# Values of two key blocks together, another order of inversions and masks, and a rearranged end in a two-layer graph network

## The chip, the cores and the metric

One core of a Trainium2 chip runs the whole program. The metric is device time of one execution in microseconds (us), the median of several. Engines are called as the profile calls them: PE is TensorE's matmul, PEld its weight load, DVE VectorE, ACT ScalarE, POOL GpSimd.

## The reference, cut to what matters

```python
# x: (32, 512, 512) float32, adj: (512, 512) of 0 and 1; 8 heads of 64
x = layernorm(x + deg * (x @ Wi.T + b) + adj @ (x @ Wj.T))     # layer 0
q, k, v = (x @ W.T + b for W, b in ...)                        # layer 1, per head
scores = q @ k.T / 8, with -inf where adj == 0
x = layernorm(x + softmax(scores) @ v @ Wo.T + bo)
```

The attention runs over 512 keys, taken as four blocks of 128.

## The kernel before

Everything is float32. The kernel is a hand-made pipeline: while the attention of one batch runs, TensorE also works on the layers of its neighbours. A **period** is one batch's attention, in eight **steps**: two groups of four heads (g = 0, 1), four key blocks each (kc). Each step has scores, values of the step before, and then **pieces**: the projections of other batches, in 8 or 16 matmul passes each, with seven products where eight would be usual.

```python
psum: mm_tile("a"), mm_tile("b")      # one bank each, for pieces
      ov_tile()  bufs=2               # one bank each, values of one head group
      sc_tile()  bufs=2               # two banks each: scores, row sums, last accumulators

def scores(b, hp, kc):                # two heads
    ps = sc_tile()
    for s in range(2):
        matmul(ps[:, s, :], KT[...64 rows...], QT[...])
    e = E[hp % 2, kc] = work([P, 2, N], "e", 4)
    nc.scalar.activation(ps, ps, AF.Exp, scale=QSCALE)       # in place, ACT
    nc.vector.tensor_tensor(e, ps, edge[...], op=OP.mult)    # the mask, DVE

def values(b, g, kc):                 # 32-column matmuls into the two ov tiles
def sums(g, ...):                     # row sums: 32-column matmuls with ones, into an sc tile
def drain(b, g):                      # ACT: sums from PSUM to SBUF
def rest(b, g):                       # DVE: four reciprocals, two scalings, one reduction
    return [(invert, g, c) for c in range(4)] + [(scale, b, g, 0), (scale, b, g, 1), (tell, b, g)]

for step in range(8):
    g, kc = divmod(step, 4)
    scores(b, 2 * g, kc); scores(b, 2 * g + 1, kc)           # with exponentials and masks
    values(pb, pg, pk)                                       # of the step before
    if pk == 3:
        sums(pg); drain(pb, pg); extra = rest(pb, pg)
    for f in PERIODS[n][step]:                               # the pieces and their helpers
        run(f)
        # after a piece: all of extra in step 0, one of it in step 4
    # ... (cuts throughout)
```

A piece ends with its **eviction**: DVE (or ACT) reads its bank (in this text the kernel's word for one 128x512 float32 tile of `psum`) and adds it into the result. The next piece but one uses that bank again.

## Time and profile before

| | before |
|---|---|
| median of the first 3 runs, us | 3696.0 (3695.5 to 3696.7) |
| PE busy | 99% |
| DVE / POOL / ACT busy | 65% / 53% / 28% |
| a period of eight steps (mean of periods 2 to 30), us | 113.46 |

The period is taken from the trace: from the first scores matmul of its first step to that of the next period. "Busy" is the union of an engine's instructions over the span. A busy share of 99% on one engine and no waits in the steady part mean that whatever costs this engine time costs the program time. The lines that carry this are in the prediction.

### The profile page before, as it was taken

What the parts mean: (1) busy time and instruction counts of PE and PEld (TensorE: products, weight loads), DVE (VectorE), ACT (ScalarE), POOL (GpSimd) and SP (SyncE); (2) the same over time, 40 slices, a digit from 0 to 9 for tenths busy, and PEclk for the clock granted to TensorE, in tenths of its full rate; (3) what the DMA queues carried; (4) which work ended last, traced back from release to release, by engine and by line L of the source; (5) the groups of instructions that cost most, each with busy time, mean ns of one, the idle gap of its engine ahead of it and who ended that gap; (6) DMA issues with size and microseconds to landing.
All of it is one profiled execution on the core that took longest, in us unless ns stands there. A gap on an engine that the chain in (4) does not pass through costs nothing.

```text
span 3693.0 us, 49640 instructions
## 1 busy us (share of the span) xinstructions
PE 3662.9 (99%) x18470; PEld 2510.3 (68%) x18470; DVE 2393.1 (65%) x3134; ACT 1028.6 (28%) x1483; POOL 1940.0 (53%) x1985
## 2 busy tenths in 40 slices
PE   9999999999999999999999999999999999999998
PEld 6766667676767676767676767676767666666663
DVE  4666666666666666666666666666666666666665
ACT  2232232222222223222223222223232322222322
POOL 3555545556445555455554555644555545555443
PEclk9999999999999999999999999999999999999999
DMA  8445556444555445564555544455545555445541
GB/s 258 141 120 140 138 154 160 139 131 135 151 157 151 129 135 146 152 165 125 135 140 151 162 144 128 136 150 155 158 123 138 142 158 159 134 133 139 148 138 44
DMA packets 797173, 530.02 MB, mean 144 GB/s; under 512 B 530432, under 2 KB 611840, under 8 KB 796928
## 3 DMA queue, kind: packets, MB, share of 16 engines
q1 hardware_dynamic: 780384, 494.78, 49.7%
q10 hardware_dynamic: 16320, 31.46, 2.3%
q8 instruction: 151, 2.47, 0.3%
q14 instruction: 94, 0.77, 0.1%
q0 software_dynamic: 224, 0.53, 0.0%
HBM read 453.25 MB, written 73.40 MB: 143 GB/s over the span
## 4 chain that ended last, share of the span: by engine, by line
PE 97%; DVE 1%; POOL 0%; DMA 0%; ACT 0%; SPq 0%; issue 0%; DVEq 0%; ACTq 0%; POOLq 0%
PE mma L436 31%; PE mmb L436 31%; PE sc L490 13%; PE ov L512 12%; PE mmb L334 4%; PE mma L334 3%; PE sc L522 2%; PE mmb L611 0%; PE mma L611 0%; DVE e L495 0%; DVE rl L531 0%; DMA xa<-hd 0%; SPq L376 0%; PE sc L736 0%; DVE st L298 0%
## 5 line engine op out<-in xcount | busy, mean ns | idle before, releaser
L494 ACT ACTIVATE sc<-sc 128x1024 f32<-128x1024 f32 x512 | 493.0, 1007 | 1554.8 <-PE sc L490 1548.8
L495 DVE TENSOR_TENSOR e<-sc,edge 128x1024 f32<-128x1024 f32 x512 | 602.6, 1218 | 205.8 <-ACT sc L494 173.3
L436 PE MATMUL mmb<-ring,big 128*128 128x256 f32 x3144 | 731.7, 381 | 0.0
L436 PE MATMUL mma<-ring,big 128*128 128x256 f32 x3112 | 724.4, 381 | 1.5 <-DVE xh L454 0.8
L436 PEld LDWEIGHTS mmb<-ring,big 128*128 128x128 f32 x3144 | 591.9, 190 | 131.6 <-issue 27.7
L436 PEld LDWEIGHTS mma<-ring,big 128*128 128x128 f32 x3112 | 585.8, 190 | 132.3 <-issue 26.5
L405 POOL TENSOR_TENSOR big<-big 128x512 f32<-128x512 f32 x376 | 492.4, 1339 | 34.5 <-DVE big L382 14.3
L490 PE MATMUL sc<-q,k 64*128 64x512 f32 x2048 | 509.4, 615 | 0.0
L512 PE MATMUL ov<-e,v 128*32 128x512 f32 x4096 | 492.4, 598 | 4.6 <-DVE oT L547 4.6
L501 POOL TENSOR_TENSOR es<-e 128x1024 f32<-128x1024 f32 x128 | 300.8, 2361 | 350.2 <-DVE e L495 350.2
L436 PE MATMUL mma<-big,ring 128*128 128x256 f32 x1808 | 430.3, 381 | 0.0
L436 PE MATMUL mmb<-big,ring 128*128 128x256 f32 x1776 | 422.8, 381 | 1.0 <-DVE v L465 1.0
L300 POOL TENSOR_SCALAR mv<-mv 128x1 f32<-128x1 f32 x256 | 49.8, 194 | 674.2 <-DVE mv L299 661.9
L436 PEld LDWEIGHTS mma<-big,ring 128*128 128x128 f32 x1808 | 340.5, 190 | 73.0 <-issue 26.0
L436 PEld LDWEIGHTS mmb<-big,ring 128*128 128x128 f32 x1776 | 334.3, 190 | 73.4 <-issue 26.0
L512 PEld LDWEIGHTS ov<-e,v 128*32 128x32 f32 x4096 | 106.9, 109 | 351.9 <-issue 320.8
L204 POOL TENSOR_TENSOR xlo<-xh,xhi 128x512 fp32r<-128x512 f32 x128 | 162.7, 1283 | 338.1 <-ACT xhi L203 338.1
L490 PEld LDWEIGHTS sc<-q,k 64*128 64x128 f32 x2048 | 176.3, 186 | 208.2 <-issue 207.0
L349 POOL TENSOR_TENSOR big<-big,deg_r 128x512 f32<-128x512 f32 x124 | 173.5, 1400 | 263.5 <-DVE big L348 263.5
L503 DVE TENSOR_TENSOR es<-es,e 128x1024 f32<-128x1024 f32 x250 | 304.8, 1220 | 0.0
L454 DVE TENSOR_TENSOR xh<-xh,mma 128x512 f32<-128x512 f32 x186 | 126.7, 681 | 263.9 <-PE mma L436 263.9
L454 DVE TENSOR_TENSOR xh<-xh,mmb 128x512 f32<-128x512 f32 x186 | 126.7, 681 | 259.2 <-PE mmb L436 259.2
(161 smaller groups left out, 3663.6 us busy)
## 6 DMA issues: line engine op xcount, KB each, us to landing
ring<-wo SPq DMA_DIRECT2D x217, 256.0 KB, 2.8
ring<-wq SPq DMA_DIRECT2D x160, 256.0 KB, 3.9
ring<-wv SPq DMA_DIRECT2D x160, 256.0 KB, 3.4
ring<-wk SPq DMA_DIRECT2D x160, 256.0 KB, 3.3
ring<-wi SPq DMA_DIRECT2D x155, 256.0 KB, 2.7
ring<-wj SPq DMA_DIRECT2D x155, 256.0 KB, 2.6
xh<-in_x_dram SPq DMA_DIRECT2D x32, 1024.0 KB, 5.4
xa<-in_x_dram SPq DMA_DIRECT2D x124, 256.0 KB, 4.0
```

Of the source, the lines that this page charges most:

```text
L204: nc.gpsimd.tensor_sub(lo, xs, hi.bitcast(FT))
L334: nc.tensor.matmul(pm, parts[w][:, jc, :], adjR[:, jc, :], start=(w == 0 and jc == 0), stop=(w == 1 and jc == NC - 1))
L349: nc.gpsimd.tensor_tensor(XD[b][:, dc, :], XD[b][:, dc, :], deg_r, op=OP.mult)
L405: nc.gpsimd.tensor_tensor(dst, p, q, op=OP.subtract)
L436: nc.tensor.matmul(pm[:, c * Q:(c + 1) * Q], lhs, rhs, start=first, stop=(kc == 1 and n == len(terms) - 1), skip_group_check=True)
L454: nc.vector.tensor_tensor(d, d, pm, op=OP.add)
L490: nc.tensor.matmul(ps[:, s, :], KT[b, hp // 2][r, hp % 2, kc * P:(kc + 1) * P], QT[b, hp // 2][r, hp % 2, :], start=True, stop=True)
L494: nc.scalar.activation(ps, ps, AF.Exp, scale=QSCALE)
L495: nc.vector.tensor_tensor(e, ps, edge[:, kc:kc + 1, :].to_broadcast([P, 2, N]), op=OP.mult)
L501: nc.gpsimd.tensor_add(ES[i], E[i, 0], E[i, 1])
L503: nc.vector.tensor_add(ES[i], ES[i], E[i, kc])
L512: nc.tensor.matmul(PV[g][r][32 * h:32 * h + 32, :], V[b][:, kc, c0:c0 + 32], E[h // 2, kc][:, h % 2, :], start=(kc == 0), stop=(kc == NC - 1))
```

## The change

The intent is to spare TensorE changes of kind. Values are made for two key blocks together, ahead of the scores of every second step. As sums and inversions then come ahead of the scores in the first step of a group, DVE's work there is put in a new order: inversions first, then the pieces' evictions, then the masks. In step 0 the masks come behind all pieces: the loop runs what stands in `late` only `if some`, and there `some = len(extra)`, which is 0 once the inversions have run. In step 4 one mask follows each of the first two pieces. The end of the program is rearranged too. The core of the diff:

```diff
     def scores(b, hp, kc):
         ...
+        nc.scalar.activation(ps, ps, AF.Exp, scale=QSCALE)
+        SC[hp] = ps
+    def mask(hp, kc):
+        ps = SC.pop(hp)
         e = E[hp % 2, kc] = work([P, 2, N], "e", 4)
-        nc.scalar.activation(ps, ps, AF.Exp, scale=QSCALE)
         nc.vector.tensor_tensor(e, ps, edge[...], op=OP.mult)
@@ the loop
-            scores(b, 2 * g, kc)
-            scores(b, 2 * g + 1, kc)
-            ... values(pb, pg, pk), sums, drain
+            alone = b == B - 1 and step > 0
+            if alone: ... scores and masks first, as before
+            if alone or kc % 2 == 0:
+                for pb, pg, pk in due:
+                    values(pb, pg, pk)
+                    if pk == NC - 1: ... sums, drain, extra = rest(pb, pg)
+                due = []
+            due.append((b, g, kc))
+            if not alone:
+                for i in range(2):
+                    scores(b, 2 * g + i, kc)
+                if kc == 0:
+                    for f in extra:            # inversions ahead of the pieces
+                        f[0](*f[1:])
+                    extra = []
+                    late = [(mask, 2 * g + i, kc) for i in range(2)]   # masks behind
+                else:
+                    for i in range(2):
+                        mask(2 * g + i, kc)
@@ phase_b: apply and store of the first half one piece earlier
@@ last batch: two key pieces moved into it, its last two pieces into step 4,
@@ the last accumulators in score tiles of their own, sums drained before the inversions
```

More of the change, by code (lines that the diff above doesn't have):

```diff
@@ L481, in piece @@
                     nc.vector.scalar_tensor_tensor(d[:, c], pm[:, c, :], bc, p1[:, c, :], op0=OP.add, op1=OP.add)
-    E, ES, PV, RL = {}, {}, {}, {}
+    SC, E, ES, PV, RL = {}, {}, {}, {}, {}
     def scores(b, hp, kc):
@@ L527, in drain, with invert @@
         nc.scalar.activation(RL[g][1], RL[g][0], AF.Identity, accum_out=told[:, j:j + 1])
-    def invert(g, part, src=1):
+    def invert(g, part):
         c = slice(part * P, (part + 1) * P)
-        nc.vector.reciprocal(RL[g][1][:, c], RL[g][src][:, c])
+        nc.vector.reciprocal(RL[g][1][:, c], RL[g][1][:, c])
     def tell(b, g):
@@ L535, in tell @@
         nc.vector.reduce_sum(told[:, j:j + 1], RL.pop(g)[1], axis=AX.X)
-    def tell_all(b, g):
-        pl, rl = RL.pop(g)
-        j = 2 * (b * 2 + g)
-        nc.gpsimd.memset(told[:, j + 1:j + 2], 0.0)
-        nc.vector.tensor_tensor_reduce(pl, pl, rl, 1.0, 0.0, OP.add, OP.add, told[:, j:j + 1])
     def scale(b, g, r, c=slice(0, N)):
@@ L568, in gnn_attention_kernel @@
     LATE = (5, 3, 6, 7, 4)
-    ALONE = ((1, "a"), (6, "b"), (2, "a"), (7, "b"), (5, "a"), (4, "b"), (3, "a"))
     def banks(n):
@@ L578, in phase_a @@
         if n == B:
-            return [pc("k", n - 1, i, bank) for i, bank in ((6, K), (5, A), (7, K), (3, A), (4, K))]
+            return [pc("k", n - 1, i, bank) for i, bank in ((5, A), (6, K), (3, A))]
         xq, aq = lambda j, m: quarter(XD[n], j, m), lambda j, m: quarter(AX_T[n], j, m)
@@ L647, in phase_b @@
         return [l0[2], *project(m, 1), l0[6], *project(m, 2), l0[7], z(add_bo, n - 1, 0), *project(m, 6), l0[4], z(stats, n, 0),
-                *project(m, 7), z(apply, n, 0), z(h_store, n, 0), l0[5], z(h_load, n, 0), z(add_bo, n - 1, 1), *project(m, 4),
+                z(apply, n, 0), z(h_store, n, 0), *project(m, 7), l0[5], z(h_load, n, 0), z(add_bo, n - 1, 1), *project(m, 4),
                 l0[3], z(stats, n, 1), z(h_turn, n, 0), *project(m, 5)]
@@ L708, in last_steps @@
         m = B - 2
-        p = {i: pc("pj", m, i, bank) for i, bank in ALONE}
+        A, K = banks(B)
+        p = {i: pc("pj", m, i, K if i in (6, 7, 4) else A) for i in ORDER}
         c = [z(combos, TO, m, ot_quarter(m), (1, 2)), z(combos, TO, m, ot_quarter(m), (3, 4))]
         own = [(4 * GA, last_part, c, 0) for c in range(2)]
-        return [[z(last_load), FLUSH, c[0], p[1], c[1]], [p[2], p[6]], [p[5], p[7], z(add_bo, B - 1, 0), z(add_bo, B - 1, 1)],
-                [p[3], p[4], z(stats, m, 0), z(stats, m, 1)], [z(apply, m, 0), z(apply, m, 1), z(store, m)], [own[0]], [own[1]], []]
+        k = [pc("k", B - 1, i, K) for i in (7, 4)]
+        return [[z(last_load), k[0], FLUSH, c[0], p[1], c[1], k[1]], [p[2], p[6]], [p[5], p[7], z(add_bo, B - 1, 0), z(add_bo, B - 1, 1)],
+                [], [p[3], p[4]], [own[0], z(stats, m, 0), z(stats, m, 1)], [own[1], z(apply, m, 0), z(apply, m, 1), z(store, m)], []]
     def run(f):
@@ L729, in last_part @@
             else:
-                t = sc_tile()
-                ACC[2], ACC[3] = t[:, 0, :], t[:, 1, :]
+                ACC[ic] = sc_tile()[:, 0, :]
         for ic in (range(2 * half, 2 * half + 2) if ic is None else (ic,)):
@@ L778, in gnn_attention_kernel @@
             g, kc = divmod(step, NC)
-            scores(b, 2 * g, kc)
-            scores(b, 2 * g + 1, kc)
-            pb, pg, pk = (b, *divmod(step - 1, NC)) if step > 0 else (b - 1, 1, NC - 1)
-            if pb >= 0:
-                values(pb, pg, pk)
-                if pk == NC - 1:
-                    sums(pg, *(((1, 3), 3) if pb == B - 1 else ()))
-                    drain(pb, pg)
-                    extra = rest(pb, pg)
-            late = [(presum, i, kc) for i in range(2) if kc > 0]
+            alone = b == B - 1 and step > 0
+            if alone:
+                for i in range(2):
[4 more added lines that the diff above has]
+                    values(pb, pg, pk)
+                    if pk == NC - 1:
+                        sums(pg, *(((1, 3), 3) if pb == B - 1 else ()))
+                        drain(pb, pg)
+                        extra = rest(pb, pg)
+                due = []
+            due.append((b, g, kc))
+            late = [(presum, i, kc) for i in range(2) if kc > 0]
+            if not alone:
+                for i in range(2):
+                    scores(b, 2 * g + i, kc)
+                if kc == 0:
[4 more added lines that the diff above has]
+                else:
+                    for i in range(2):
+                        mask(2 * g + i, kc)
             if b == B - 1 and kc > 2 - g:
@@ L808, in gnn_attention_kernel @@
     sums(1, (3,), 3)
-    for c in range(2):
-        last_part(c, 1)
+    drain(B - 1, 1)
     for ic in range(NC):
         c = slice(ic * P, (ic + 1) * P)
-        invert(1, ic, 0)
+        invert(1, ic)
         scale(B - 1, 1, 0, c)
         scale(B - 1, 1, 1, c)
+        if ic < 2:
+            last_part(0, 1, ic + 2)
+            last_part(1, 1, ic + 2)
         last_part(2, ic=ic)
@@ L819, in gnn_attention_kernel @@
             last_rows(ic - 1)
-    tell_all(B - 1, 1)
+    tell(B - 1, 1)
     last_rows(NC - 1)
```

## The prediction

Marked cuts take out what no trace or run of this case shows: rules on the engines and their memory, and with them the amount that rival (c) put on a wait and its total. The forecast's own sum: 3696 - 16 + 68 + 31 + 6 - 5 = 3780, put at 3778.

> **What bounds the kernel now.** I read the page first: busy time and the chain that ended last. One engine fills the span.
>
> ```profile
> PE 3662.9 (99%) x18470; PEld 2510.3 (68%) x18470; DVE 2393.1 (65%) x3134; ACT 1028.6 (28%) x1483; POOL 1940.0 (53%) x1985
> ...
> PE 97%; DVE 1%; POOL 0%; DMA 0%; ACT 0%; SPq 0%; issue 0%; DVEq 0%; ACTq 0%; POOLq 0%
> ```
>
> TensorE (PE) is busy 3662.9 of 3693.0 us and is 97% of the chain; VectorE (DVE), 65%, carries nothing that ends last. So only two things can move the time: fewer TensorE nanoseconds, or new waits of TensorE. Its waits today, the largest rows of the waits filtered to PE:
>
> ```profile
> PE ov L512 <- DVE oT L547: 4.6, 3, 2.7
> PE ov L750 <- DVE tot L748: 4.3, 1, 4.3
> PE sc L522 <- DVE e L495: 2.2, 2, 2.0
> ```
>
> The "ov" and "sc" waits lie after 3570 us, in the last batch, and the L750 one is the flag test at the very end. The 31 periods before it hardly wait. The chain in order of time shows what a step costs (start, length, what, matmul passes):
>
> ```profile
> 1018.50 1.92 PE sc L490 x8
> 1020.41 1.85 PE ov L512 x16
> 1022.27 3.65 PE mmb L436 x16
> 1025.92 1.73 PE mma L436 x8
> 1027.65 3.45 PE mmb L436 x16
> ```
>
> Scores (sc), values (ov), then pieces of the projections. Sixteen passes cost 3.65 us straight after values and 3.45 otherwise: a change of kind costs 0.20. The row sums, in values' own shape, take 0.86 for 8 passes in the same view, so 16 should be 1.72; values take 1.85: 0.13 to enter them. Scores, at the same pace, 1.92 for 1.72: 0.20.
>
> [...] scores use 64 rows, values 32 columns, pieces the whole array, and each change costs 0.13 to 0.20 us. [...] DVE stood 1.41 us for a load before a transpose at 1288.24 with the next work behind it. [...] Here the clock fell to 0.91 only in 3640:3660, with its 2.73 us wait.
>
> **The change, part by part.**
>
> *Pairing.* Two steps now enter scores, values and pieces twice: 2 x (0.20 + 0.13 + 0.20) = 1.06 us. Afterwards: values (0.13), scores (0.20), pieces (0.20), scores (0.20), pieces (0.20) = 0.93. I assume an entry costs the same whatever came before; entering values from pieces is in no trace yet. Pairs: 3 in the first batch, 30 x 4, one at the head of the last: 124. Gain 124 x 0.13 = 16 us. Matmuls are the same.
>
> *Inversions ahead of pieces, masks behind them.* In the first step of each group of heads (steps 0 and 4 of eight) the four reciprocals, two scalings and one reduction go to DVE at once, ahead of piece evictions, and the two masks later. A mask reads a score tile; with two such tiles the next step's scores cannot start until it is done. In the built program the instruction order is clear: in step 0, DVE stands as reciprocals x4, scale x2, reduction, eviction, eviction, eviction **of the step's last piece**, mask, mask; and the first scores matmul of step 1 waits for the first of these masks. Today the masks stand right behind the exponentials and evictions are behind them. Costs, from the timeline of DVE before:
>
> ```profile
> 1238.76 0.69 DVE L454 TENSOR_TENSOR xh<-xh,mmb 128x512 f32<-128x512 f32 x1 [3.81 <-PE mmb L436]
> 1239.37 3.38 DVE L531 RECIPROCAL rl<-rl 128x128 f32<-128x128 f32 x4
> 1242.78 1.29 DVE L547 TENSOR_TENSOR oT<-ov,rl 128x512 f32<-128x512 f32 x2
> 1243.98 0.68 DVE L535 TENSOR_REDUCE told<-rl 128x1 f32<-128x512 f32 x1
> 1244.58 0.68 DVE L454 TENSOR_TENSOR xh<-xh,mmb 128x512 f32<-128x512 f32 x1
> 1245.79 0.69 DVE L454 TENSOR_TENSOR xh<-xh,mma 128x512 f32<-128x512 f32 x1 [0.54 <-PE mma L436]
> 1247.83 2.36 DVE L495 TENSOR_TENSOR e<-sc,edge 128x1024 f32<-128x1024 f32 x2 [1.35 <-ACT sc L494]
> ```
>
> Start to start: an eviction occupies 0.61, the inversion block 1239.37 to 1244.58 = 5.2, a mask 1.22 (two 2.36).
>
> Step 0 to 1: the last piece's eviction starts about 0.49 after its last matmul starts (1018.61 against 1018.12 in the records). Then 0.61 eviction, 1.22 mask, 0.04 to TensorE = 2.36; scores would have started 0.31 after that matmul. **Wait 2.05 us.** The second score tile needs the second mask, 1.14 later, where 0.96 of matmuls lie between: 0.2 more. About **2.2 us**, 31 times: 68 us.
>
> Step 4, counted from the first scores matmul: these follow the sums directly now. TensorE: scores 1.92, then pieces k 1.83, q 1.73, v 1.73, so the next q piece, which adds into the first q's bank, could start at 7.20. DVE: the row sums are drained and the first reciprocal starts at 0.85 (today 1.83 after the sums begin, which take 0.98 themselves); + 5.2 = 6.06; one mask 1.14; q's eviction 0.88; 0.04: 8.12. **Wait 0.92 and a 0.10 restart: 1.0 us**, 31 times: 31 us. The timeline before shows how it was avoided:
>
> ```profile
> 1296.99 0.88 DVE L481 SCALAR_TENSOR_TENSOR q<-mma,bq_c,p 128x256 f32<-128x256 f32 x2 [1.95 <-PE mma L436]
> 1297.78 0.94 DVE L531 RECIPROCAL rl<-rl 128x128 f32<-128x128 f32 x1
> ```
>
> an eviction the moment its piece is ready, one reciprocal between two evictions.
>
> *Odd steps without values.* Their pieces start 1.85 us nearer to the scores, while DVE's masks start when they did. In step 7 before (scores at 1331.07) the k eviction starts at 1339.63 and ends 9.24 after the scores began; the piece that needs that bank will come at 9.15: a wait of 0.1 to 0.2. I carry 0.2 x 31 = 6 us. In step 4 the drain of the sums ends 0.85 after the scores begin and the second score tile is wanted at 0.96: hidden.
>
> *The end.* Score tiles one by one for the last accumulators, two pieces moved into the last batch, two to its step 4. Before, rows of the last two blocks start their statistics at 3680.71 and 3683.74, the second behind ScalarE's read of the first, because both share a tile. Separate tiles and interleaving should save some 4 us there. The moves save perhaps 2 of the 2.0 + 2.7 us waits, but the last batch's step 0 gets its own mask wait (2.2) and a bank wait (1.4). The earlier waits of the last two periods (0.7 and 1.0) should go too. Net 5 us gained, an estimate.
>
> *The earlier apply and store* only moves a transpose's load earlier: neutral.
>
> Sum: 3696 - 16 + 68 + 31 + 6 - 5 = **3780**; I put 3778, as the waits may absorb one another a little.
>
> **The rivals.** (a) *The drains saved show in full and DVE keeps up*: 3696 - 16 - 5 = 3675, "same". For it: DVE is only 65% busy and the intent is this. Against it: [...] the mask stands behind an eviction that cannot start before the step's matmuls end. (b) *Only step 0 waits*; step 4 is hidden because ScalarE or the banks leave more room: 3696 - 21 + 68 = 3743, within 2%. (c) *Waits of 2 us lower the TensorE clock*: matmuls after each wait then run slowly[...]. Against it: the 2.0 us wait at 3637 left the clock at 1.00. (d) *Pool or DMA becomes the bound*: Pool is 53% busy and nothing is added to it; no.
>
> **Range and chances.** Two per cent is 3770. The waits' sum, 105 us, is uncertain by some 25 either way: a tenth of a microsecond per period is 3 us; the drains by 8, the end by 5. That gives 3745 to 3806. Point 3778 is just above the line, so slower 0.68, within 0.30, faster 0.02.
>
> **What would show it.** In the waits of PE: "sc (scores) from DVE e", about 60 times, 60 to 75 us in all, longest near 2.1; "mma and mmb (pieces) from DVE q", about 31 times near 0.9. TensorE's busy time should fall by some 15 us while the span grows. In the chain in order of time: values x32 at 3.57 (3.44 + 0.13), followed by scores at 1.92; pieces right after scores 1.92 for 8. DVE's timeline: masks of step 0 behind three evictions. If these score waits are absent, or hidden by matmuls, the prediction is wrong and (a) holds; if they exceed 2.5 us, a mask is waiting on more than one eviction.

## The result, and the profile after

| | before | changed |
|---|---|---|
| median of 6 runs, us | 3695.4 | 3837.2 |
| range | 3692.3 to 3696.7 | 3833.4 to 3838.2 |
| ratio | | 1.0384 (95%: 1.0371 to 1.0397) |
| PE busy, us | 3662.9 | 3703.8 |
| granted clock, mean | 0.998 | 0.990 |

A ratio here is the mean time of one kernel's fast runs over that of the other's of the same rounds, so not quite the ratio of the medians. The change is slower by 3.8%. The direction was predicted; the size was not: 3837 lies over the range.

The page of the changed kernel, busy time and chain:

```profile
PE 3703.8 (97%) x18470; PEld 2521.6 (66%) x18470; DVE 2385.8 (62%) x3133; ACT 1040.9 (27%) x1485; POOL 1953.3 (51%) x1984
...
PE 75%; DVE 15%; issue 4%; POOL 4%; ACT 2%; DMA 0%; DVEq 0%; SPq 0%; POOLq 0%; ACTq 0%
```

The same 18470 matmul records, yet DVE now has 15% of the chain where it had 1%: TensorE follows DVE. The waits of PE say at which places (total, times, longest):

```profile
PE sc L490 <- DVE e L499: 66.6, 33, 3.7
PE mmb L436 <- DVE q L481: 12.2, 15, 0.8
PE mma L436 <- DVE q L481: 11.4, 14, 0.8
PE mmb L436 <- DVE k L474: 6.2, 17, 1.2
```

The first row is step 1's scores waiting for step 0's masks, the second and third step 4's q piece, the fourth mostly step 7's key piece. The timelines of DVE, then PE, of one step 0:

```profile
1298.95 0.69 DVE L454 TENSOR_TENSOR xh<-xh,mma 128x512 f32<-128x512 f32 x1 [1.04 <-PE mma L436]
1299.56 2.35 DVE L499 TENSOR_TENSOR e<-sc,edge 128x1024 f32<-128x1024 f32 x2
```

```profile
1296.96 1.89 PE L436 MATMUL mma<-ring,oT 128*128 128x256 f32 x8
1300.83 2.26 PE L490 MATMUL sc<-q,k 64*128 64x512 f32 x8 [1.98 <-DVE e L499]
```

The step's last piece, its eviction at 1298.95, the two masks from 1299.56, and only then, at 1300.83, the scores of step 1. The gap between the starts of the last piece's last matmul and the first scores matmul is 2.36 us in the records where 0.31 is usual.

What the change was made for did arrive. The chain in order of time:

```profile
1313.65 3.57 PE ov L516 x32
1317.22 1.92 PE sc L490 x8
1319.13 3.65 PE mmb L436 x16
```

32 passes of values in 3.57 us are 3.44 + 0.13: entering them from pieces costs what it costs from scores.

To see every place at once, I measured each step in the trace, from its first scores matmul to the next step's, and took means over periods 2 to 30. "Matmuls alone" is worked out from the kernel before: its step, less the 1.85 us of values that left it, with 3.57 for the pair that now stands at its end and the 0.86 of sums moved with it. For step 1 that is 14.33 - 1.85 + 3.57 = 16.05.

| step | before | matmuls alone | changed | excess |
|---|---|---|---|---|
| 0 | 15.24 | 12.53 | 14.56 | 2.03 |
| 1 | 14.33 | 16.05 | 17.18 | 1.13 |
| 2 | 14.33 | 12.48 | 12.48 | 0.00 |
| 3 | 14.33 | 16.91 | 17.18 | 0.27 |
| 4 | 13.48 | 10.77 | 11.85 | 1.08 |
| 5 | 14.33 | 16.05 | 16.05 | 0.00 |
| 6 | 14.68 | 12.83 | 12.83 | 0.00 |
| 7 | 12.73 | 15.31 | 15.83 | 0.52 |
| sum | 113.46 | 112.93 | 117.95 | 5.03 |

The pairing is worth 0.53 us per period, the waits cost 5.03. Over the 29 periods that is 130 us of the 143 by which the profiled spans differ. The first period is 15.8 us longer (118.2 against 102.4), the last period and the last batch together 2.9 us shorter.

Step 1's 17.18 is a mean of two kinds: 16.32 in some periods, about 17.9 in others. The granted clock tells them apart. Two stretches right after such a wait:

```profile
1300.80:1304.20 3.40, 3.37 (x13) 1.00 0.06 20
1418.20:1421.60 3.40, 3.40 (x9) 0.60 0.04 16
```

The last three columns are granted clock, DMA share and GB/s. In the second stretch TensorE started 9 matmuls instead of 13. The trace's clock records hold 21 half-clock stretches in this execution, against 2 before; the steady ones last 3.41 us, and all begin at the same phase of a 3.41 us grid, whose cells I call **windows**. Of the steps 1 of the 31 periods, 17 took about 17.9 us, and the first 19.9. I took each stand in front of step 1's scores (a **stand** is the time in which TensorE starts nothing, counted from 0.22 us after the last matmul's start; usually 2.15 us in all), cut it by that grid, and took the largest share that it filled of one window. At 0.53 or more the next window was at half clock, at 0.49 or less it was not, without exception among 32 stands. The traces of e3_order_only and e8_masks_behind (below), worked the same way, give 0.51 and 0.48 in 64 more stands. This tells of the first slow window only: in the first period a second one followed, of which the runs do not show the cause.

### The profile page after: what moved, and what is told of

Read it like the earlier page. It is cut to its first block, busy times and chain, and to the rows that moved or that the text cites. A ratio compares the mean times of both kernels' runs of the same rounds, so it can differ in the third digit from the quotient of the medians.

```text
span 3836.4 us, 49707 instructions
## 1 busy us (share of the span) xinstructions
PE 3703.8 (97%) x18470; PEld 2521.6 (66%) x18470; DVE 2385.8 (62%) x3133; ACT 1040.9 (27%) x1485; POOL 1953.3 (51%) x1984
## 4 chain that ended last, share of the span: by engine, by line
PE 75%; DVE 15%; issue 4%; POOL 4%; ACT 2%; DMA 0%; DVEq 0%; SPq 0%; POOLq 0%; ACTq 0%
PE mma L436 24%; PE mmb L436 24%; PE ov L516 12%; PE sc L490 10%; DVE e L499 4%; DVE xh L354 3%; DVE rl L535 3%; POOL xlo L204 2%; PE sc L526 2%; PE mmb L334 1%; DVE oT L544 1%; POOL big L349 1%; DVE k L474 1%; DVE es L507 1%; PE mma L334 1%
## 5 line engine op out<-in xcount | busy, mean ns | idle before, releaser
L436 PE MATMUL mma<-ring,big 128*128 128x256 f32 x3112 | 734.3, 385 | 4.9 <-PE sc L490 3.4
L490 PE MATMUL sc<-q,k 64*128 64x512 f32 x2048 | 536.4, 639 | 66.7 <-DVE e L499 66.6
L516 PE MATMUL ov<-e,v 128*32 128x512 f32 x4096 | 467.9, 596 | 2.1 <-DVE oT L544 2.1
L535 DVE RECIPROCAL rl<-rl 128x128 f32<-128x128 f32 x256 | 217.3, 910 | 218.7 <-ACT rl L531 218.7
L204 POOL TENSOR_TENSOR xlo<-xh,xhi 128x512 fp32r<-128x512 f32 x128 | 175.9, 1386 | 340.6 <-ACT xhi L203 340.6
L516 PEld LDWEIGHTS ov<-e,v 128*32 128x32 f32 x4096 | 119.8, 109 | 277.4 <-issue 274.1
L305 ACT ACTIVATE xh<-xh,mv 128x512 f32<-128x512 f32 x252 | 194.3, 809 | 374.7 <-POOL mv L302 363.9
```

The costliest lines, as they stand in the source:

```text
L204: nc.gpsimd.tensor_sub(lo, xs, hi.bitcast(FT))
L305: nc.scalar.activation(y, y, AF.Identity, bias=mv[:, 4:5], scale=mv[:, 3:4])
L436: nc.tensor.matmul(pm[:, c * Q:(c + 1) * Q], lhs, rhs, start=first, stop=(kc == 1 and n == len(terms) - 1), skip_group_check=True)
L490: nc.tensor.matmul(ps[:, s, :], KT[b, hp // 2][r, hp % 2, kc * P:(kc + 1) * P], QT[b, hp // 2][r, hp % 2, :], start=True, stop=True)
L516: nc.tensor.matmul(PV[g][r][32 * h:32 * h + 32, :], V[b][:, kc, c0:c0 + 32], E[h // 2, kc][:, h % 2, :], start=(kc == 0), stop=(kc == NC - 1))
L535: nc.vector.reciprocal(RL[g][1][:, c], RL[g][1][:, c])
```

## The experiments

Theory A: **the order** inside the first step of a group makes the waits, and the clock adds to them. Rival B: **pairing** makes them, as pieces now follow closer on the scores in steps without values. Rival C, for the part beyond my forecast: no clock effect, only more waits. Ten kernels ran, all correct. Times are medians; "before" is the kernel before in the same rounds, and the interval is that of the ratio.

### e2_pair_only: the old order, with pairing

```diff
-                if kc == 0:
-                    for f in extra:
-                        f[0](*f[1:])
-                    extra = []
-                    late = [(mask, 2 * g + i, kc) for i in range(2)]
-                else:
-                    for i in range(2):
-                        mask(2 * g + i, kc)
+                for i in range(2):
+                    mask(2 * g + i, kc)
```

> The changed kernel with the pairing and the new end kept, but the order of the kernel before inside the first step of a group: masks right behind the exponentials, inversions behind the first piece. Theory (the order makes the waits): the 2.05 us wait of step 1's scores and the 1.1 us of step 4 go, and with them the half-clock windows; what stays is 0.5 us in step 7 and 0.27 in step 3 per period, perhaps 0.3 new in step 0, less 0.54 for the drains saved: about 3710 us. Rival (pairing itself, pieces too near to the scores, makes the loss): stays over 3780.

Measured: 3708.7 us, ratio 1.0039 (1.0022 to 1.0056). Its largest wait rows in the steady part:

```profile
PE mmb L436 <- DVE k L474: 4.7, 16, 0.8
PE mma L436 <- DVE k L474: 4.0, 15, 0.6
```

The scores' and q's rows of the changed kernel are gone: step 0 takes 12.55 us, step 4 10.77, as the matmuls alone. What stays is step 7 (15.83), step 3 (17.13) and 0.14 in step 5. So 128 of the 143 us belong to the order, and pairing with the new end still loses 15 us of time against the kernel before, 9 of them in the first period.

### e3_order_only: the new order, without pairing

```diff
-            alone = b == B - 1 and step > 0
+            alone = b == B - 1 and step > 0 or kc != 0
```

> The order alone: values of every block on their own again, but in the first step of a group values, sums, scores, inversions, pieces, and masks behind them, as in the changed kernel; new end kept. Theory (order): step 0 to 1 costs 3 us per period with the clock's half windows, step 4 1.1, the first period some 13: about 3830 us, nearly as slow as the changed kernel. Rival (pairing): about 3700.

Measured: 3819.9 us, ratio 1.0339 (1.0322 to 1.0357).

```profile
PE sc L490 <- DVE e L499: 66.6, 33, 3.7
PE mmb L436 <- DVE q L481: 12.2, 15, 0.8
PE mma L436 <- DVE q L481: 11.4, 14, 0.8
```

To the tenth the rows of the changed kernel, with no pair in the program. Steps 3 and 7 take what their matmuls take (17.04 and 15.44 in this arrangement). Rival B is out for the bulk; it keeps steps 3 and 7, 0.79 us per period, more than the 0.53 gained.

### e1_masks_front: masks first, inversions still ahead of pieces

```diff
+                for i in range(2):
+                    mask(2 * g + i, kc)
                 if kc == 0:
                     for f in extra:
                         f[0](*f[1:])
                     extra = []
-                    late = [(mask, 2 * g + i, kc) for i in range(2)]
-                else:
-                    ...
```

> The changed kernel with only the masks of the first step of a group moved to the front, the inversions still ahead of the pieces and now behind the masks. If the masks' place alone is at fault, the time falls to about 3740. My theory is that the 5.2 us block of inversions in front of the evictions is as harmful as the masks behind them: with masks first, the first piece's eviction ends 10.5 us after the scores began and the third piece wants the bank at 7.2, 3.3 us in step 0 and 3.5 in step 4 per period, against 4.2 removed: about 3915, slower than the changed kernel, more if the clock halves more often.

Measured: 4043.7 us (4024.6 to 4067.3), ratio 1.0935 (1.0876 to 1.0994). The chain in a step 4:

```profile
1289.22 2.36 DVE e L499 x2
1291.57 3.31 DVE rl L535 x4
...
1296.78 0.80 DVE q L481 x2
1297.58 0.04 issue
1297.62 3.78 PE mmb L436 x8
```

Masks, inversions, scalings, and only then q's eviction, for which the piece at 1297.62 waited; it then took 3.78 us for 8 passes that take 1.73 at 1308.21 in the same chain, as at half clock. The direction was right, the size was short by 128 us. The waits came about as expected: TensorE stands 3.10 us in step 0 and 3.24 in step 4 of a steady period. The clock is enough for the rest: its mean was 0.955 of full speed, against 0.990 in the changed kernel. The records hold 56 half-clock stretches against 21, most of them 6.83 us long instead of 3.41, and TensorE was busy for 315 us in them against 71 in the changed kernel. In the changed kernel's slow stretches piece passes start 0.43 us apart, and 0.22 elsewhere. By that the work would take half the time at the full clock, so the stretches cost some 157 us against 35 (an estimate from these records). The author's order is better than this one: with inversions ahead of the pieces, masks must go behind. The inversions had better not be there.

### e8_masks_behind: masks behind, inversions as before

```diff
                 if kc == 0:
-                    for f in extra:
-                        f[0](*f[1:])
-                    extra = []
                     late = [(mask, 2 * g + i, kc) for i in range(2)]
+                    if g == 0:
+                        tail, late = late, []      # run behind the whole step
```

> The changed kernel with only half of its order: masks of step 0 behind all its pieces and those of step 4 behind its first two, but the inversions back among the pieces as in the kernel before. Step 0's wait of 2.05 us and what follows in step 1 (0.27, and 1.58 where the clock halves) should stay, step 4's 1.1 us should go: 3709 + 31 x 3.05 + some 6 in the first period = about 3805. If the inversions ahead were what holds step 0 too, it falls to about 3710.

Measured: 3823.0 us, ratio 1.0352 (1.0336 to 1.0368), 18 us over my figure. Step 0 takes 14.67, step 1 16.93 and step 4 11.09: the wait behind the masks stays, step 4's shrinks from 1.08 to 0.32, and step 5 pays 0.32 for leftover inversions. Against e2_pair_only the masks' place costs 114 us; adding the inversions' place costs 14 more. Of the two parts of the order, **the masks behind the last eviction of step 0** are nearly all.

### e4_fill and e11_fill_half: does a wait cost more than its length?

```diff
             if not alone:
+                if step == 1:
+                    fill = ov_tile(), ov_tile()
+                    for _ in range(4):             # 2 in e11_fill_half
+                        nc.tensor.matmul(fill[0][:, :Q], ident, bo_r[:, :Q], start=True, stop=True)
                 for i in range(2):
                     scores(b, 2 * g + i, kc)
```

> The changed kernel with four idle matmuls of 128x128 by 128x256 (1.73 us) put into the wait in front of the scores of every step 1; their result is read by nobody. They fill 1.73 of the 2.05 us, so by the waits alone the time stays at 3837. If the waits also cost through the clock (half rate for one 3.41 us window in 17 of 31 periods, 1.58 us each), step 1 falls from 17.9 to 16.3 us in those periods and the time to about 3810, with no half-clock window left at step 1 but in the first period.

> The changed kernel with half the filling: two idle matmuls (0.86 us) ahead of the scores of every step 1. TensorE then stands some 1.2 us, a third of a 3.41 us clock window. In the changed kernel's trace the clock halved where the wait filled 0.53 of one window or more and not at 0.49 or less; if that is the rule, no step 1 but the first period's is at half clock, and the time is that of the full filling, 3811. If any wait of about a microsecond can halve the clock, it lies between 3811 and 3837.

Measured: 3811.5 us (ratio 1.0318, 1.0301 to 1.0336) and 3810.5 us (1.0313, 1.0297 to 1.0328). The same wait row in the two kernels, full filling first:

```profile
PE sc L490 <- DVE e L499: 13.1, 33, 2.2
```

```profile
PE sc L490 <- DVE e L499: 39.9, 33, 2.8
```

Work that nobody reads makes the program 26 us faster, and step 1 takes 16.32 us in every steady period of both, 17.9 in none. With half the filling TensorE still stands 1.28 us each time in the steady periods, which is at most 0.38 of a window (one period reached 0.47), and the clock holds. So a stand in front of step 1's scores that filled at most 0.49 of any one window cost its length, and one that filled 0.53 or more of one (0.51 in the traces of e3 and e8) cost 1.6 us more (17.9 against 16.32). Rival C is out.

### e5_end_only: the new end alone

```diff
-            alone = b == B - 1 and step > 0
+            alone = True
```

> The new end alone: no pairing, every step in the order of the kernel before; two key pieces moved into the last batch, separate score tiles for the last accumulators, store of the first half one piece earlier. From the run with pairing alone, periods 31 and the last together took 188.8 us against 194.0 of before, of which 0.7 is pairing: about 4.5 us gained, 3689. If the new end gives nothing by itself, 3694.

Measured: 3690.4 us, before 3693.4; ratio 0.9990 (0.9977 to 1.0004). Within the noise; the profiled spans differ by 4.8 us and its periods 31 and last take 189.0 us against 194.0. The end does no harm and perhaps some good.

### e6_best: a version meant to beat both, first try

To e2_pair_only: the first batch unpaired, step 7's second update of the base behind its last transpose, and step 2's transpose ahead of the statistics.

```diff
-            alone = b == B - 1 and step > 0
+            alone = b == B - 1 and step > 0 or b == 0
-            if i in (1, 2):
-                res += [z(base, n, i - 1)]
+            if i in (1, 3):
+                res += [z(base, n, i // 2)]
-                l0[3], z(stats, n, 1), z(h_turn, n, 0), *project(m, 5)]
+                l0[3], z(h_turn, n, 0), z(stats, n, 1), *project(m, 5)]
```

> A version to beat both: pairing and new end, masks and inversions in the order of the kernel before, first batch unpaired, the transpose of step 2 ahead of the statistics, and the second base update behind the last transpose of step 7. Of the 3709 us of pairing with the old order, 0.27 (step 3) and 0.5 (step 7) per period and some 6 us of the first period should go: about 3679. If the two waits only move elsewhere, it stays near 3702; a gain over the kernel before (3694) of 0.4% is what the 124 saved changes of kind are worth.

Measured: 3716.4 us, ratio 1.0062 (1.0048 to 1.0076): a miss. Step 7 fell from 15.83 to 15.30, the 15.31 of its matmuls, so its excess was those base updates ahead of an eviction on DVE. The first period fell from 111.8 to 105.3. But step 3 rose from 17.13 to 17.98, by a new wait:

```profile
PE mma L436 <- ACT p L443: 11.4, 15, 1.1
PE mmb L436 <- ACT p L443: 10.6, 15, 1.1
```

In DVE's timeline the transpose now stood 1.85 us for its load and held up the statistics behind it; ACT's normalization waits for what follows from those (`ACT xh L305 <- POOL mv L302`: 382.0 us in 110 waits) and stands in front of the copy that frees a bank.

### e9_safe and e10_best: the bad move taken back, and a better one

e9_safe takes that move back and lets the first piece of step 4 take two inversions. e10_best also puts the projection piece of step 3 ahead of the first value piece, exchanges some later pieces, and puts the transpose behind the eviction of step 2's last piece.

```diff
# both, to e6_best
-  ... else max(1, round(f[0] / PC))
+  ... else max(1, round(f[0] / PC)) + (len(extra) == 7)
# e9_safe
-                l0[3], z(h_turn, n, 0), z(stats, n, 1), *project(m, 5)]
+                l0[3], z(stats, n, 1), z(h_turn, n, 0), *project(m, 5)]
# e10_best
-                l0[3], z(h_turn, n, 0), z(stats, n, 1), *project(m, 5)]
+                l0[3], z(stats, n, 1), *project(m, 5), z(h_turn, n, 0)]   # kept in the same step
-  v[1], *project(m, 3), z(h_load, n, 1), z(stats, m, 0), v[2], z(stats, m, 1), q[1], k[1], ..., q[2]
+  *project(m, 3), v[1], z(h_load, n, 1), z(stats, m, 0), q[1], z(stats, m, 1), v[2], q[2], ..., k[1]
```

> The version before it (3716) with its one bad move taken back: the transpose of step 2 again behind the statistics, where the trace shows it starting just as its load lands; and the first piece of step 4 takes two inversions, so that step 5 starts without a leftover. Step 3 should fall from 17.98 to 17.12 us and step 5 from 16.19 to 16.05: 3716 - 30 x 1.0 = 3686, a little under the kernel before (3693). If it stays over 3693, the gain of the pairing is eaten by waits that I have not found.

> As the run beside it, and the last wait of a period taken out too: in step 3 the projection piece goes ahead of the first value piece, with its bank freed ahead of the transpose, so that the transpose's load has 1.8 us more. Step 3 should fall from 17.12 to 16.9 us, the sum of a period to 112.9 against 113.46 of the kernel before: 3693 - 30 x 0.54 - 3 (the end) = 3674. If a bank or an eviction now waits, step 3 stays over 17.1 and the time near 3686.

Measured in the same rounds as a kernel before of 3694.6: e9_safe 3681.1 us, ratio 0.9966 (0.9953 to 0.9980); e10_best 3676.8 us, ratio **0.9951 (0.9938 to 0.9965)**. The page of e10_best:

```profile
PE 3645.8 (99%) x18470; PEld 2513.2 (68%) x18470; DVE 2385.1 (65%) x3133; ACT 1037.8 (28%) x1485; POOL 1990.7 (54%) x1984
```

TensorE is busy 17 us less than before, at 99% again. A period takes 112.99 us, against 112.93 for its matmuls alone. Both beat the kernel before by a little, and the changed kernel by 4%.

| mean of periods 2 to 30, us | before | changed | e2 | e8 | e6 | e9 | e10 |
|---|---|---|---|---|---|---|---|
| step 0 | 15.24 | 14.56 | 12.55 | 14.67 | 12.55 | 12.55 | 12.55 |
| step 1 | 14.33 | 17.18 | 16.05 | 16.93 | 16.05 | 16.05 | 16.05 |
| step 3 | 14.33 | 17.18 | 17.13 | 17.17 | 17.98 | 17.14 | 16.98 |
| step 4 | 13.48 | 11.85 | 10.77 | 11.09 | 10.77 | 10.77 | 10.77 |
| step 5 | 14.33 | 16.05 | 16.19 | 16.37 | 16.19 | 16.05 | 16.05 |
| step 7 | 12.73 | 15.83 | 15.83 | 15.81 | 15.30 | 15.30 | 15.30 |
| period | 113.46 | 117.95 | 113.82 | 117.34 | 114.14 | 113.15 | 112.99 |

## Why the prediction was right about the waits and wrong about the clock and the sum

- **What bounds it**: right. Only TensorE's own time and its new waits moved the program; DVE stayed under 65%.
- **Gain of pairing, 16 us**: right. 0.53 per period was measured, 0.52 forecast; e10_best shows 17 us less busy time.
- **Step 0 to 1, 2.2 us per period**: right. The wait was 2.05, with 0.27 more in step 1 (0.2 forecast). e8_masks_behind shows that it comes with the masks' place alone, e3_order_only that it needs no pairing.
- **Step 4, 1.0 us**: right, 1.08. e8_masks_behind took most of it away by moving the inversions back. The 0.10 for a restart is in the trace before: after the wait that ends at 127.13 the second pass starts 0.32 us after the first, where 0.22 is usual.
- **Odd steps**: the term was mis-sized. I carried 0.2 for step 7 alone; it was 0.52, and step 3 had 0.27 that I had no term for. I had taken step 7 from a single period's timeline, and passed over step 3, where a transpose stands in front of the first value piece. Over 29 periods this is 17 us. e6_best showed the base updates as step 7's cause. e10_best, which moves that piece with several others, shows that step 3's wait can be removed (16.98 us), not which of the moves did it.
- **The clock**: this step failed, by a misreading. The prediction set its rival (c) aside: "Against it: the 2.0 us wait at 3637 left the clock at 1.00." It did not. That wait ended at 3639.74; one of the two half-clock stretches of the trace before begins at 3640.23 and lasts 3.41 us (the other, 10.42 us, begins at 3684.60, at the end of the 4.30 us wait before the last matmuls), and the row sums behind the wait took nearly twice what as many passes took later in the same chain:

```profile
3639.74 3.24 PE sc L522 x16
3662.97 1.72 PE sc L522 x16
```

The view that was read had windows of 20 us. A border at 3640 put the slow stretch beside the 2.73 us wait, which began at 3645.2 and halved nothing. By the wait rows and this trace's grid the first wait filled 0.59 of one window and the second 0.54 (3645.23 to 3647.06), yet the clock was 1.00 in the window behind the second (3647.06 to 3650.47). So what was measured on the stands in front of step 1's scores does not hold for every wait: why this one halved nothing the runs do not show. But the trace on hand held a wait of 2.00 us with a slow stretch behind it, which spoke for (c). In the changed kernel the clock halved in 17 of 31 steps 1, besides the first, at 1.6 us each, about 26 us; the two fillings gave back 26. (c) charged every period, and lacked the odd steps above and the first period below.
- **The first period**: I counted it as one of "31 times". It lost 15.8 us instead of 2.9. Its mask wait was the longest (3.7 us), its step 1 took 19.9 us, with two half-clock windows in a row, and in steps 2 and 3 normalization's transposes, which share the score tiles, waited 1.9 us for ACT and 1.8 for DVE. In e2_pair_only that period still takes 111.8 us; unpaired in e6_best it takes 105.3, which is the 102.4 of before plus, but for 0.2 us, the values and sums that moved across its border.
- **The end, 5 us gained**: periods 31 and last were 2.9 us shorter, of which I had expected one usual period's loss; about right in sum.

What I had missed, in us: the clock 26, the first period 13, steps 3 and 7 another 17, and a few hundredths per period in steps 1 and 4 some 5. Together that is 61, where 59 lay between 3778 and the measured time. The clock alone does not explain the miss: with it taken out, e4_fill still measures 3811, over the range's end of 3806.

"What would show it" held in part. The score waits came to 66.6 us, within the 60 to 75 forecast, but in 33 waits and not about 60, the longest 3.7 us (in the first period) and not 2.1. Those for q were 29 (about 31 forecast), 23.6 us. Busy time was to fall by some 15 us and rose by 41. The half-clock stretches hold 71 us of busy time against 4 before, so matmuls that count as busy for longer make up about 33 us of that difference (an estimate). The other 24 or so lie in steps 1, 3, 4 and 7, whose recorded busy time, slow windows apart, is 0.84 us per period over their matmuls alone: part of a wait stands in the records as busy.

## What to carry to other kernels

On an engine whose timeline shows its work in the program's order, as DVE's does here (it stood 1.41 us for a transpose's load at 1288.24 in the trace before, its next work behind it), put behind one another only what becomes ready in that order: here a mask of 1.22 us behind the eviction of a piece not yet done held TensorE up for 2.05 us, with DVE busy 62%. Before moving helper work away from one place, list for each tile who waits for its release, and look in every step, the first round too. When TensorE must wait, see whether the clock records show slow stretches behind the waits, and look at them one by one, not in a mean over 20 us. If they do, shorter waits can pay twice: here stands of 1.28 us left the clock alone, and matmuls that nobody read made the program faster.
